# Moving the logits tile of the second layer from the attention's tile pool to the kept residual's pool

## The chip, the cores and the metric

The kernel is one launch on one core of a Trainium2 chip. The metric is device time in microseconds (us). TensorE is called PE (its weight loads PEld), VectorE DVE, ScalarE ACT, GpSimd POOL and SyncE SP. "L1098" is line 1098 of the kernel's source.

## The reference, cut to what matters

Two layers run over x, 2708 tokens of 256 floats, with a 2708 x 2708 adjacency matrix. Each layer is a graph attention followed by a top-2 mixture of 8 experts, both added to the residual. The change lies in the second layer:

```python
# layer 1, attention (x is the residual, Xn its layer norm)
H = Xn @ W_fc + b_fc
scores = where(adj > 0, s_src[:, None] + s_dst[None, :], -1e9)
x = x + softmax(scores) @ H
# layer 1, experts
xf = layernorm(x)
logits = xf @ gate_w + gate_b              # [2708, 8]
probs = softmax(logits); top2_vals, top2_idx = top_k(probs, 2)
for e in range(8):                          # hidden size 512
    y = gelu(xf @ W1[e] + b1[e]) @ W2[e] + b2[e]
    acc += weight_of(e) * y
x = x + acc
```

Since the row's own score s_src cancels in the softmax, the kernel weights row j of H with exp(s_dst[j]). And since the gate is linear, the gate's 8 columns are folded into the matrix of the attention: each value row carries its share of the logits, and the attention sums them with the rest.

## The kernel before, in words

Tokens are handled in 22 tiles t of 128 rows (the last has 20). Layer 0 ends with its experts, whose results are scattered into xd0 in memory. Then `layer1_attention` runs, and after it `experts1.run`.

**Attention of layer 1.** It opens a tile pool att1 (L585) on the left side of SBUF. In it lie parts (the value rows as three bf16 parts), logits (L589, 22 x 8 floats for each partition), spread_of, e_tail, sums_of and the working tiles xT, e, rest, m_tail. The residual rows lie in `kept`, in a pool of their own on the right side (L1226), which is open to the end of the kernel. While the first group of tiles is under way, every tile t gets its norm, its columns and its values; L624 writes the part of `logits[:, t]` that comes from the token itself. The 22 tiles are attended in groups of 6, 6, 4, 3 and 3 (GROUPS). When a group is done, L682 copies its sums out of PSUM to `raw`, and a generator `finish` (L665) for each tile is put into a list of open work, `line`. At L722 the loop ends; its pools are closed when `layer1_attention` returns, while the finishes of the last groups are still open in `line`.

**finish and route.** Each call of `line.step()` moves every open finish on by one step. Its steps for layer 1: divide by the sum (L234 to L239), add into kept (L670), add the attention's share to `logits[:, t]` (L673), norm statistics (L197 to L199, with a power on POOL in L203), the normalized row (L209), the scaled logits (L865, the last read of `logits[:, t]`), the two best experts (L870, L871), the softmax over them (L876, L877 on ACT), the one-hot sum `sel` (L887), two matmuls that count places (L891, L892), and two indirect DMAs from POOL which scatter the row to its experts (L909).

**Experts of layer 1.** Rows are worked off in slots of 128 rows of one expert, 47 here. After 16 routed tiles `begin` (L1020) places slots 0 to 23, and asks for rows and weights of the first three. The weights lie in a ring of four buffers, which were filled ahead with guessed experts; `fetch_weights` (L1047) is an indirect DMA from POOL whose indices are out of bounds, and move nothing, where the right expert is there already. A slot is `up` (L1085): two transposes of its rows to PSUM (L1088), a copy to `xe` (L1098), a copy of the bias (L1101), 16 matmuls (L1108), 4 Gelu (L1116); then `down` (L1121) of the slot before: 8 matmuls (L1124), y (L1130, L1131), and a scatter to xd1 (L1135). Between them stand two `line.step()`. When `line` is empty, `place(24, SLOTS)` lays out the remaining slots. The tiles xe, bias2, hT and y come from the pool ffn2, called two (L1074), which is opened on the right side after att1 is closed. Its PSUM pools (L1075 to L1077) take the banks of the attention's.

**What sets the order.** SP's instructions keep the order of the source. On the other engines, the tile framework lays out an order at build time: an instruction that is earlier in the source goes first if its inputs are there by the framework's own estimate of time. On the chip each engine then works through its list in that order, and waits on semaphores. A pool that takes the addresses of an earlier pool comes after it: in the built program, xe of slot 0 lies at bytes 147712 to 148736 of a partition, att1 at 112000 to 158144, and logits at 145408 to 146112. xe of slot 0 shares no byte with logits, yet its copy (L1098) carries a semaphore wait on the DVE's own count, and the value is that of L865 of tile 21.

Of the kernel before, what the change touches and what calls it, by code (L numbers as in the profile page):

```python
# [9 lines left out]
F32 = mybir.dt.float32  # L10
# [9 lines left out]
P = 128  # L20
# [3 lines left out]
E = 8  # L24
BN = 512
EPS = 1e-5
NT = (N + P - 1) // P
# [33 lines left out]
def adj_ffn_kernel(ctx: ExitStack, tc: tile.TileContext, a: dict, out: bass.AP):  # L61
# [521 lines left out]
    def layer1_attention(mTs, kept, line):  # L583
        with ExitStack() as scope:
            pool = scope.enter_context(tc.tile_pool(name="att1", bufs=2))  # L585
            ps_acc = scope.enter_context(tc.tile_pool(name="acc1", bufs=6, space=PSUM))
            parts = pool.tile([P, NT - 1, 3, VALUES + 1], BF16, name="parts", bufs=1)

            logits = pool.tile([P, NT, E], F32, name="logits", bufs=1)  # L589
            spread_of = pool.tile([P, NT], F32, name="spread_of", bufs=1)  # L590
            e_tail = pool.tile([P, VALUES + 1], F32, name="e_tail", bufs=1)
            sums_of = pool.tile([P, DC, NT], F32, name="sums_of", bufs=1)
# [623 lines left out]
    with tc.tile_pool(name="mask", bufs=1) as mp:  # L1216
        mTs = [
            mp.tile([P, NT, nb], FP8, name=f"mT{b}") for b, (_, nb, _) in enumerate(BLOCKS)
        ]
        background.extend(  # L1220
            partial(nc.sync.dma_start, mTs[b], neighbours[b][:]) for b in range(len(BLOCKS))
        )
        experts0.run(line)
        early_rows.close()

        kept_pool = ctx.enter_context(tc.tile_pool(name="kept", bufs=1, side="right"))  # L1226
        kept = kept_pool.tile([P, NT, D], F32, name="kept")
        layer1_attention(mTs, kept, line)
# [58 lines left out]
```

## Time and profile before

| what | value |
|---|---|
| device time, median of 3 runs | 1366.69 us (1365.86 to 1366.7) |
| device time of the profiled execution | 1365.33 us |
| its span from first to last instruction | 1363.6 us |
| PE busy in the span | 1251.6 us (92%) |
| DVE, POOL, ACT busy | 581.8, 413.1, 333.5 us |
| mean TensorE clock granted | 0.962 |
| last matmul of the attention (L661) ends | 1108.67 us |
| first expert matmul of layer 1 (L1108) starts | 1122.39 us |

Times of single instructions are counted from the span's start. In a timeline, a line gives start, duration, engine, source line, operation, output and inputs, count, and in brackets the idle time before it with what ended that. In a table of windows, each engine has its busy time in that stretch and the number of instructions; PEclk is the granted clock as a share of full speed. Since the profile is of one execution, sums of its durations are taken against its own 1365.33 us; the 1.7 us outside of the span stay as they are.

### The profile page before, as it was taken

To read this page: it belongs to the slowest core of one execution; us is meant where nothing else is said; L and a number is where in the kernel's file an instruction comes from. 1 tells how busy PE (TensorE), PEld (TensorE's weight loads), DVE (VectorE), ACT (ScalarE), POOL (GpSimd) and SP (SyncE) were. 2 spreads that over 40 slices of the span, in tenths; PEclk is the share of its full clock that TensorE was granted. 3 is DMA by queue.
4 is the path that set the end of the run, shared out by engine and by line. 5 is a ranking of instruction groups with operands and counts; after the bars stand their busy time and mean duration, and the time that the engine had idled before them with its cause. 6 is when DMAs were issued, how large, how long until landed. Compare 5 with 4: busy or idle time off the path is not lost. (4 is left out here: it accounts for less than half of the span.)

```text
span 1363.6 us, 21427 instructions
## 1 busy us (share of the span) xinstructions
PE 1251.6 (92%) x7536; PEld 975.8 (72%) x7536; DVE 581.8 (43%) x2261; ACT 333.5 (24%) x1008; POOL 413.1 (30%) x521
## 2 busy tenths in 40 slices
PE   7999999999999999999999999689999868999980
PEld 4666666666566666999999999567887637888860
DVE  5723743636427255512212222276636564333324
ACT  3222212212112223533333233134100003222220
POOL 5200110110111112533333333341144365544440
PEclk8899999999999999999999999889999879999995
DMA  7701355988928327375678454440010033536447
GB/s 215 248 5 40 117 168 132 257 226 222 251 74 186 98 95 283 73 241 157 183 250 292 118 165 130 108 176 1 1 48 29 30 104 122 176 101 226 156 156 252
DMA packets 106058, 201.39 MB, mean 148 GB/s; under 512 B 25633, under 2 KB 79990, under 8 KB 99418
## 3 DMA queue, kind: packets, MB, share of 16 engines
q1 hardware_dynamic: 75740, 109.41, 28.1%
q0 software_dynamic: 27392, 87.78, 20.3%
q10 hardware_dynamic: 2814, 2.77, 0.6%
q8 instruction: 62, 1.02, 0.3%
q14 instruction: 50, 0.41, 0.1%
HBM read 263.63 MB, written 66.12 MB: 242 GB/s over the span
## 5 line engine op out<-in xcount | busy, mean ns | idle before, releaser
L1124 PE MATMUL acc<-ring,hT 128*128 128x256 f32 x1096 | 272.4, 385 | 16.7 <-ACT hT L1116 9.4
L1108 PEld LDWEIGHTS mm<-xe,ring 128*128 128x128 f32 x2192 | 266.8, 195 | 17.3 <-issue 8.3
L1108 PE MATMUL mm<-xe,ring 128*128 128x128 f32 x2192 | 274.9, 280 | 4.4 <-DVE xe L1098 3.4
L1116 ACT ACTIVATE hT<-mm,ring 128x128 f32<-128x128 f32 x548 | 156.4, 369 | 358.6 <-issue 337.5
L1124 PEld LDWEIGHTS acc<-ring,hT 128*128 128x128 f32 x1096 | 194.3, 191 | 45.5 <-issue 13.2
L429 PE MATMUL s<-g,xnT 128*128 128x512 f32 x420 | 206.4, 607 | 6.0 <-DVE mT L441 6.0
L486 PE MATMUL acc<-v,p 128*128 128x257 f32 (+1 forms) x880 | 209.1, 389 | 0.0
L1130 DVE TENSOR_TENSOR y<-acc,bias 128x256 f32<-128x256 f32 x92 | 39.1, 425 | 323.3 <-PE acc L1124 317.6
L655 PE MATMUL acc<-parts,mT 128*128 128x265 bf16 (+1 forms) x1386 | 173.0, 281 | 0.4 <-DVE raw L682 0.3
L486 PEld LDWEIGHTS acc<-v,p 128*128 128x128 f32 (+1 forms) x880 | 153.0, 190 | 18.0 <-issue 0.8
L1049 POOL DMA_INDIRECT ring<-L_ffn_packed,weight_row x98 | 102.8, 1049 | 206.5 <-issue 92.0
L655 PEld LDWEIGHTS <-mT 128*128 128x128 fp8e4 (+1 forms) x1386 | 132.3, 98 | 45.9 <-issue 18.7
L203 POOL TENSOR_TENSOR ln_rs<-ln_rs,minus_half 128x2 f32<-128x2 f32 x88 | 68.1, 776 | 242.2 <-DVE ln_rs L199 210.9
L441 DVE TENSOR_SCALAR mT<-s 128x512 fp8e4<-128x512 f32 x105 | 72.0, 687 | 138.8 <-ACT p L440 138.7
L909 POOL DMA_INDIRECT disp<-row,to x88 | 87.5, 994 | 137.8 <-DVE to L906 52.8
L429 PEld LDWEIGHTS s<-g,xnT 128*128 128x128 f32 x420 | 76.1, 193 | 53.3 <-issue 42.7
L440 ACT ACTIVATE p<-s 128x512 f32<-128x512 f32 x105 | 62.2, 595 | 168.1 <-PE s L435 167.0
L1142 POOL DMA_INDIRECT xd<-y,xg x45 | 70.7, 1571 | 82.8 <-issue 34.8
L435 PEld LDWEIGHTS <-apart 128*128 128x128 fp8e4 x420 | 32.5, 98 | 60.4 <-issue 60.4
L324 DVE TENSOR_SCALAR apart<-adj 128x677 fp8e4<-128x677 int32 x80 | 40.8, 515 | 47.9 <-DMA adj<-in_adj_dram 47.6
L1135 POOL DMA_INDIRECT xd<-y,xg x47 | 47.2, 1004 | 24.0 <-issue 11.3
L877 ACT ACTIVATE p<-p 128x2 f32<-128x2 f32 (+3 forms) x44 | 9.1, 206 | 163.1 <-DVE p L876 85.2
(227 smaller groups left out, 1126.1 us busy)
## 6 DMA issues: line engine op xcount, KB each, us to landing
adj<-in_adj_dram SPq DMA_DIRECT2D x84, 338.5 KB
L_ffn_packed<-in_L_ffn_W_dram SPq DMA_DIRECT2D x16, 1024.0 KB
xg<-disp SPq DMA_DIRECT2D x98, 129.0 KB
L_ffn_packed<-in_L_ffn_W_dram SPq DMA_DIRECT2D x16, 512.0 KB
neighbours<-mT SPq DMA_DIRECT2D x5, 1408.0 KB
mT<-neighbours SPq DMA_DIRECT2D x5, 1408.0 KB
xin<-in_x_dram SPq DMA_DIRECT2D x42, 128.0 KB
ring<-L_ffn_packed SPq DMA_DIRECT2D x4, 1154.0 KB
```

Of the source, the lines that this page charges most:

```text
L203: nc.gpsimd.tensor_tensor(rs[:r, 1], rs[:r, 0], minus_half[:r], ALU.pow)
L429: nc.tensor.matmul(ps[:kr, :nb], xnT[:, c, k0 : k0 + kr], g[:, c, :nb], start=(c == 0), stop=False,)
L440: nc.scalar.activation(p[:kr, :nb], ps[:kr, :nb], AF.Exp, scale=1.0 / 16.0)
L441: nc.vector.tensor_scalar(mT[:kr, k, :], ps[:kr, :nb], -BIG / 2, None, ALU.is_gt, saturate=False,)
L486: nc.tensor.matmul(accs[j][:r], p[keys, q0 : q0 + r], v[keys, k, :], start=(k == 0), stop=(k == NT - 1),)
L655: nc.tensor.matmul(acc[:r], mT[:, k, j * P : j * P + r], parts[:, k, i], start=(k == 0 and i == 0), stop=False,)
L909: nc.gpsimd.indirect_dma_start(disp[:], bass.IndirectOffsetOnAxis(ap=to[:r, j : j + 1], axis=0), rows2[j][:r], None,)
L1049: nc.gpsimd.indirect_dma_start(w, None, packed[:], bass.IndirectOffsetOnAxis(ap=self.weight_row[:, s : s + 1], axis=0), bounds_check=E * P ...
L1108: nc.tensor.matmul(ps[:, i, :], w[:, c * hidden + f * P : c * hidden + (f + 1) * P], xe[:, c, :], start=(c == 0), stop=(c == DC - 1),)
L1116: nc.scalar.activation(hT[:, f, :], ps[:, i, :], AF.Gelu, bias=w[:, b1 + f : b1 + f + 1])
L1124: nc.tensor.matmul(ps, hT[:, f, :], w[:, w2 + f * D : w2 + (f + 1) * D], start=(f == 0), stop=(f == hc - 1),)
L1142: start = nc.gpsimd.indirect_dma_start(xd[:], at, y, None, bounds_check=N - 1, oob_is_err=False, compute_op=ALU.add)
```

## The change

One line: the tile of the logits is taken from the pool of kept, with the same shape and type. That pool has one buffer for each tile, and is on the right side of SBUF; 22 x 8 x 4 = 704 bytes of each partition move from the left side to the right. All reads and writes of logits stay what they are.

```diff
             ps_acc = scope.enter_context(tc.tile_pool(name="acc1", bufs=6, space=PSUM))
             parts = pool.tile([P, NT - 1, 3, VALUES + 1], BF16, name="parts", bufs=1)
 
-            logits = pool.tile([P, NT, E], F32, name="logits", bufs=1)
+            logits = kept_pool.tile([P, NT, E], F32, name="logits")
             spread_of = pool.tile([P, NT], F32, name="spread_of", bufs=1)
```

## The prediction

> **What bounds the kernel now.** I read the page first: PE is busy for 92% of the span, so only time in which PE stands, or runs at a low clock, can be won. Then I asked for busy time in stretches of 20 us around the end of the second attention, where the logits are last used.
>
> ```profile
> 1080.00:1100.00 20.00, 20.00 (x152) 11.28 (x150) 11.87 (x76) 1.48 (x8) 9.16 (x14) 1.00 0.10 34
> 1100.00:1120.00 20.00, 10.38 (x73) 5.80 (x72) 13.26 (x79) 0.68 (x3) 12.20 (x17) 0.76 0.41 135
> 1120.00:1140.00 20.00, 17.80 (x112) 16.50 (x112) 9.57 (x51) 6.35 (x21) 11.78 (x16) 0.82 0.22 67
> ```
>
> After the time come the busy times of PE, PEld, DVE, ACT and POOL, then the clock. PE works throughout until 1100, does half of the next 20 us, and comes back at a clock of 0.82. So there is a hole of some 10 us, with a slow start behind it. The timeline of PE shows its edges:
>
> ```profile
> 1110.29 0.66 PE L1088 MATMUL tp<-ident,xg 128*128 128x128 f32 x2 [1.45 <-DMA xg<-disp]
> ...
> 1113.63 0.17 PE L892 MATMUL misc<-seen,ones 128*128 128x8 bf16 x1 [1.89 <-DVE raw L239]
> 1121.74 0.17 PE L891 MATMUL misc<-sel,before 128*128 128x8 bf16 x1 [7.94 <-DVE sel L887]
> 1121.76 0.17 PE L892 MATMUL misc<-seen,ones 128*128 128x8 bf16 x1
> 1122.39 6.17 PE L1108 MATMUL mm<-xe,ring 128*128 128x128 f32 x32 [0.47 <-DVE xe L1098]
> ```
>
> Slot 0's rows are transposed by 1110.95, but its first matmul starts at 1122.39. The brackets blame sel of tile 19 for 7.94 us; the end of the hole is xe. The DVE's timeline says why xe is so late:
>
> ```profile
> 1117.44 0.41 DVE L209 TENSOR_SCALAR row<-kept,ln_mv,ln_rs 128x256 f32<-128x256 f32 x1 [2.29 <-POOL ln_rs L203]
> ...
> 1121.33 0.21 DVE L865 SCALAR_TENSOR_TENSOR lg<-logits,ln_rs,L_ffn_gate_b_b 20x8 f32<-20x8 f32 x1 [2.41 <-POOL ln_rs L203]
> 1121.47 0.21 DVE L887 TENSOR_TENSOR sel<-hot 128x8 bf16<-128x8 f32 x1
> 1121.61 0.39 DVE L209 TENSOR_SCALAR row<-kept,ln_mv,ln_rs 128x256 f32<-128x256 f32 x1
> 1121.93 0.41 DVE L1098 COPY xe<-tp 128x256 f32<-128x256 f32 x1
> ```
>
> The 20-row line is the last read of logits (tile 21). xe follows it as the built program demands: its wait is on just that L865. L865 waited for POOL's power, and POOL was full:
>
> ```profile
> 1108.73 1.07 POOL L1049 DMA_INDIRECT ring<-L_ffn_packed,weight_row  x1 [0.64 <-DVE raw L682]
> 1110.10 1.23 POOL L1049 DMA_INDIRECT ring<-L_ffn_packed,weight_row  x1 [0.30 <-issue]
> ...
> 1116.68 1.55 POOL L203 TENSOR_TENSOR ln_rs<-ln_rs,minus_half 128x2 f32<-128x2 f32 x2
> ...
> 1120.58 0.72 POOL L203 TENSOR_TENSOR ln_rs<-ln_rs,minus_half 20x2 f32<-20x2 f32 x1
> ```
>
> So today's order is POOL's power for tile 21, L865, release of att1, xe, expert matmuls. From there to 1329 the experts keep PE at about 18.4 of every 20 us; an earlier start moves the end of the kernel, as the tail (results scattered, read back, added, stored) hangs on the last slot.
>
> **What the Trainium skill says.** "TensorE: Matmul & The Clock Gate", section "What's actually happening": PE runs at half clock until it has been busy for some 3.4 us. The trace agrees in kind: the clock is 1.00 until 1110, 0.50 from 1112 to 1126, and 0.84 in the next 4 us. "ScalarE: Activation LUTs", section "What ACT_TABLE_LOAD costs": about 1283 ns for each switch, plus some 1380 ns of draining. The trace has the same 1283 ns; the drain isn't visible in it as a group. No page says when a tile pool's memory is free; that is a matter of the built program.
>
> **The change, part by part.**
>
> *Removed wait.* With logits elsewhere, att1's last users are the matmuls that read parts, m_tail and e_tail. The last (L661) ends at 1108.67, before slot 0's transposes. xe(0) is then bound by these, 1110.95. DVE has no gap from 1108.15 to 1115.15, so the copy comes between other instructions (each at most 0.48 us): done by about 1112. Its weights are there: the request of 1108.73 moved nothing (the DMA view has only small packets on POOL's queue until 1112). So the matmuls of slot 0 start at about 1112.0 instead of 1122.39; 10.4 us is the ceiling, 11 with the copy first in line.
>
> *What is late next: slot 1's weights.* The DMA view by microsecond has, on POOL's queue, 0.15 MB in 1112 to 1113, 0.43 MB in 1113 to 1114 and 0.60 MB in 1114 to 1116, in sum 1.18 MB, which is one ring buffer (128 x 2308 x 4 bytes). It starts a microsecond after the second request ends (1111.33): I take it that slot 1's guess was wrong. So slot 1 can't start before 1116.0. Slot 0's 16 matmuls at half clock take 3.6 us (15 of the 32 took 1122.39 to 1125.75), so to 1115.6; slot 1 from 1116.0 to 1119.5. From the end of slot 1's matmuls to the start of slot 2's there are 2.7 us before (1128.56 to 1131.25; transposes, half of down(0), Gelu). So slot 2 starts at 1122.2 instead of 1131.25: 9.0 us gained without new waits. The half clock is paid in both kernels; I give it no gain.
>
> *Routing of tiles 19 to 21 now lies beside slots.* (a) PE's L891 of tile 19 needs sel, which DVE gives at 1121.7, since POOL is no faster. If it stands right behind slot 1's matmuls, PE waits from 1119.5 to 1121.7: 2.2 us; if later, nothing. I take 1.3. DVE's y(0) and xe(2) queue behind L865 of tile 21 until 1121.5, and are needed at about 1121.5: nothing. (b) ACT did the three Exp (L877, at 1118.86, 1123.77, 1125.54) before its first Gelu, with one table load. Now they alternate: up to three switches there and back, 3 x 2 x 1.28 = 7.7 us (double with the drains of the page). ACT needs 1.15 of 3.85 us for each slot, so 2.7 us a slot are free and a Gelu is due only after the next slot's 2 us of matmuls. Bounds: 0 to 7.7; I take 0.7, since at most one Gelu at a time lies behind a switch. (c) POOL gets two more requests for each slot, 1.04 + 1.02 + gaps = 2.7 us, into a queue that is full until 1125. The routing scatters come later by up to three slots, 8 us; the next that needs them all is the placing of slots 24 on, in slot 5, and a weight request is made three slots (11.5 us) ahead. Nothing, if the order holds; bounds -3 to +4 us, as PE already loses about 5 us around that placing (slot 4 starts at 1138.98, slot 6 at 1153.53, for a pitch of 3.85).
>
> *Moved memory.* The first write of logits (L624) must now find kept's addresses free. kept's own first load comes earlier in the same pool, and DVE waited 8.7 us for it; L624's group shows 5.4 us of idle time, all but a trace of it for ACT's e. So nothing. Left and right sides shift by 704 bytes and stay clear of each other by the same gap. No instruction, DMA or queue entry is added; DVE, ACT and PE do the same work.
>
> Sum: 9.0 - 1.3 - 0.7 = 7.0 us. Against the profiled execution 1365.33 - 7.0 = 1358.3; its time is 1.4 below the median of the runs, so for the median 1366.69 - 7.0 = **1359.7**.
>
> **The rivals.**
> 1. *PE's order keeps the routing ahead of slot 1.* If the build places L891 of tile 19 before slot 1's matmuls, these start at 1121.8, end at 1125.2, slot 2 starts at 1127.9: 3.4 us gained, 1363.3. For it: the build does not know that slot 0's weights move nothing, so its estimate of weight arrival may be late. Against: slot 1 is earlier in the source, and PE is idle by then.
> 2. *The wait stays.* Some other late tile of att1, or the PSUM pools, holds two back; then 1366.7. Against: the wait of xe names L865 of tile 21, and only logits is read by finish and route from att1.
> 3. *Slower: ACT's queue.* An Exp stands before a Gelu and waits for its softmax input, which waits for POOL, now fuller by 2.7 us a slot. Each of three Exp then costs two switches with drains (5.3 us) and, with PE waiting for hT, up to 4 us of it are seen by PE: 12 against the 9 won, so 1369.7. It decides from 3 us seen per Exp. Against: 2.7 us of each slot are free on ACT.
> 4. *The hole around the placing closes too:* it costs 5 us now, and a different order may lose less; 1366.69 - 7 - 4 = 1355.7.
>
> **How the numbers follow.** Forecast 0.50, rival 1 0.25, rival 2 0.10, rival 3 0.10, rival 4 0.05. A measurement can tell about 0.2%, 2.7 us, from no change: faster are the forecast, rival 4 and most of rival 1 (3.4 lies close to the bound, so 0.03 of it goes to the middle), 0.77; same 0.13; slower 0.10. The range leaves out rivals 2 and 3: from 1355.5 (ceiling of 11 us, and rival 4) to 1365.5.
>
> **What would show it.** Right: xe(0) on DVE before the last L865, the first L1108 near 1112, slot 1 at 1116 to 1117, PE busy about 17 of 20 us in 1100 to 1120, more ACT table loads than the 10 of the groups before, the last matmul some 7 us earlier. Wrong: xe(0) still behind L865 (rival 2); L891 with a long idle bracket before slot 1 (rival 1); waits of L1124 for hT (rival 3); or a later stall around the placing that takes the gain back.

## The result and the profile after

| | kernel before | changed kernel |
|---|---|---|
| median of 6 runs each | 1366.7 us (1365.86 to 1369.49) | 1373.59 us (1369.48 to 1377.27) |
| ratio, with its 95% interval | | 1.0047 (1.0026 to 1.0067) |
| profiled execution, span | 1363.6 us | 1375.5 us |

The changed kernel is slower by about 6 us, where 7 us less were forecast. A second comparison on another chip (run e5 below) gave 1.0031 (1.0016 to 1.0045). The chips differ by some us, and single executions of one kernel on one chip by up to 16, so from here on times are compared as ratios to the kernel before on the same chip, and profiles from one fixed point: the end of the attention's last matmul (L661), which in the changed kernel's profile is at 1110.86 and in the one before at 1108.67.

What was forecast for the start of the experts came. DVE copies xe of slot 0 long before the last read of the logits:

```profile
1113.23 0.42 DVE L1098 COPY xe<-tp 128x256 f32<-128x256 f32 x1 [0.60 <-issue]
...
1138.95 0.20 DVE L865 SCALAR_TENSOR_TENSOR lg<-logits,ln_rs,L_ffn_gate_b_b 20x8 f32<-20x8 f32 x1
```

The windows show a full PE from 1100 to 1140 (16.82 against 10.38 in the first of these stretches), and then a hole in 1140 to 1160, where the kernel before had 16.30 us of PE:

```profile
1100.00:1120.00 20.00, 16.82 (x107) 10.71 (x105) 12.50 (x67) 1.82 (x3) 11.12 (x14) 0.83 0.43 138
1120.00:1140.00 20.00, 18.26 (x115) 16.88 (x116) 10.09 (x63) 9.20 (x27) 10.86 (x13) 0.91 0.17 48
1140.00:1160.00 20.00, 7.25 (x47) 5.87 (x45) 7.99 (x41) 3.55 (x8) 14.23 (x16) 0.82 0.52 168
```

PE's timeline has the start, the hole, and what follows it:

```profile
1114.78 3.62 PE L1108 MATMUL mm<-xe,ring 128*128 128x128 f32 x16
...
1121.09 0.41 PE L1088 MATMUL tp<-ident,xg 128*128 128x128 f32 x2 [2.34 <-DMA xg<-disp]
...
1121.37 3.24 PE L1108 MATMUL mm<-xe,ring 128*128 128x128 f32 x16
...
1160.75 3.78 PE L1124 MATMUL acc<-ring,hT 128*128 128x256 f32 x8 [12.11 <-ACT hT L1116]
...
1178.47 1.95 PE L1108 MATMUL mm<-xe,ring 128*128 128x128 f32 x16
1180.26 0.38 PE L1088 MATMUL tp<-ident,xg 128*128 128x128 f32 x2
1180.93 1.99 PE L1124 MATMUL acc<-ring,hT 128*128 128x256 f32 x8 [0.29 <-issue]
1182.76 0.27 PE L1088 MATMUL tp<-ident,xg 128*128 128x128 f32 x1
1182.87 1.95 PE L1108 MATMUL mm<-xe,ring 128*128 128x128 f32 x16
```

Two things are to be seen here. One is loud: 12.11 us before the down of slot 6. The other is quiet: after the hole each down (L1124) stands right behind its own up (L1108) and waits for the Gelu, 0.29 to 0.51 us in every slot, and the pitch of the slots (the time from one slot's start to the next) is 4.3 to 4.4 us. The page shows the loud part, not the quiet one. The first line is the group of the down in the kernel before, the second in the changed one:

```profile
L1124 PE MATMUL acc<-ring,hT 128*128 128x256 f32 x1096 | 272.4, 385 | 16.7 <-ACT hT L1116 9.4
```

```profile
L1124 PE MATMUL acc<-ring,hT 128*128 128x256 f32 x1096 | 273.0, 386 | 29.0 <-ACT hT L1116 22.9
```

The idle time for hT grows from 9.4 to 22.9 us, and 12.11 us of that is the one hole. The order of PE's list shows in the pitch.

POOL's timeline shows a changed order. Slot 4's weights go into the buffer of slot 0. Their request now stands ahead of the powers of tiles 19 and 20 (L203), and waits for slot 0's down, so the powers come at 1129.42 and not at 1116.68:

```profile
1117.85 0.98 POOL L909 DMA_INDIRECT disp<-row,to  x1 [0.31 <-issue]
1127.05 1.04 POOL L1049 DMA_INDIRECT ring<-L_ffn_packed,weight_row  x1 [8.22 <-PE acc L1124]
...
1129.42 1.42 POOL L203 TENSOR_TENSOR ln_rs<-ln_rs,minus_half 128x2 f32<-128x2 f32 x2
```

From there to 1158 POOL sends one indirect request after the other, and in the middle of that SP's eight stores of the placing take 16.21 us from 1143.89 on (6.33 before).

To see where the lead went, I took from each profile the starts of the slots (first of the 16 matmuls L1108), counted from the end of L661. Runs e1 to e18 are told below; e1 has the engine order of the kernel before in these slots, e5 is the changed kernel again.

The lead of a kernel at a slot is how much earlier that slot starts than in the kernel before.

| start of slot | before | e1 | changed | e5 | e11 serial | e9 | e10 |
|---|---|---|---|---|---|---|---|
| 2 | 22.6 | 22.6 | 16.2 | 13.6 | 22.3 | 13.5 | 22.5 |
| 4 | 30.3 | 30.3 | 24.1 | 21.4 | 30.0 | 20.7 | 30.6 |
| 6 | 44.9 | 39.3 | 35.7 | 36.4 | 45.1 | 33.5 | 40.9 |
| 8 | 52.6 | 46.7 | 58.9 | 52.7 | 54.6 | 51.1 | 50.8 |
| 12 | 68.3 | 62.2 | 76.3 | 70.1 | 71.8 | 68.9 | 67.0 |
| 24 | 120.1 | 114.1 | 128.5 | 122.3 | 123.2 | 116.5 | 115.9 |
| end of PE | 224.4 | 218.4 | 234.2 | 227.9 | 228.3 | 218.5 | 217.5 |

At slot 4 the changed kernel is 6 to 9 us ahead of the kernel before in its two profiles. At slot 8 it is 6 behind in the first and level in e5; at slot 12 it is 8 and 2 behind, and it loses 1 to 2 us more from there to the end. So nearly all is decided in slots 4 to 11.

### The profile page after: what moved, and what is told of

It reads as the page before. It is cut to its first block, busy times and chain, and to the rows that moved or that the text cites. A ratio compares the mean times of both kernels' runs of the same rounds, so it can differ in the third digit from the quotient of the medians.

```text
span 1375.5 us, 21421 instructions
## 1 busy us (share of the span) xinstructions
PE 1253.2 (91%) x7536; PEld 978.4 (71%) x7536; DVE 581.6 (42%) x2261; ACT 338.9 (25%) x1012; POOL 412.9 (30%) x521
## 5 line engine op out<-in xcount | busy, mean ns | idle before, releaser
L1124 PE MATMUL acc<-ring,hT 128*128 128x256 f32 x1096 | 273.0, 386 | 29.0 <-ACT hT L1116 22.9
L1108 PE MATMUL mm<-xe,ring 128*128 128x128 f32 x2192 | 276.7, 281 | 2.9 <-DVE xe L1098 2.9
L1108 PEld LDWEIGHTS mm<-xe,ring 128*128 128x128 f32 x2192 | 268.3, 196 | 15.4 <-issue 7.1
L1124 PEld LDWEIGHTS acc<-ring,hT 128*128 128x128 f32 x1096 | 195.8, 192 | 60.2 <-ACT hT L1116 28.6
L486 PEld LDWEIGHTS acc<-v,p 128*128 128x128 f32 (+1 forms) x880 | 154.3, 192 | 18.3 <-issue 0.8
L203 POOL TENSOR_TENSOR ln_rs<-ln_rs,minus_half 128x2 f32<-128x2 f32 x88 | 67.8, 773 | 244.4 <-DVE ln_rs L199 213.1
L846 POOL COPY row<-token 128x1 int32<-128x1 int32 (+1 forms) x88 | 17.1, 207 | 101.1 <-DMA disp<-row,to 99.8
```

Source lines behind the costliest of these rows:

```text
L203: nc.gpsimd.tensor_tensor(rs[:r, 1], rs[:r, 0], minus_half[:r], ALU.pow)
L486: nc.tensor.matmul(accs[j][:r], p[keys, q0 : q0 + r], v[keys, k, :], start=(k == 0), stop=(k == NT - 1),)
L1108: nc.tensor.matmul(ps[:, i, :], w[:, c * hidden + f * P : c * hidden + (f + 1) * P], xe[:, c, :], start=(c == 0), stop=(c == DC - 1),)
L1124: nc.tensor.matmul(ps, hT[:, f, :], w[:, w2 + f * D : w2 + (f + 1) * D], start=(f == 0), stop=(f == hc - 1),)
```

## The experiments

The first theories were: **A**, the early start brings the placing and POOL's late routing scatters together; **B**, the moved addresses cost by themselves; **C**, ACT's alternation of Exp and Gelu; **D**, POOL's burst alone.

**e1: the old wait put back.**

```diff
-            logits = kept_pool.tile([P, NT, E], F32, name="logits")
+            logits = kept_pool.tile([P, NT, E], F32, name="logits"); experts1.gate_bias = pool.tile([P, E], F32, name="bias_copy", bufs=1); nc.vector.tensor_copy(experts1.gate_bias, gb_b)
```

> The changed kernel, with the old wait put back by other means: L865 adds a copy of the gate's bias that lies in att1 (one DVE copy of 128x8 more), so the attention's pool is again free only after L865 of tile 21, while logits stays in kept's pool. Theory A (the loss comes from what the earlier start of the slots does to the order of the work around the placing of slots 24 on): the old order comes back and with it the old time, 1366.7 within 2. Theory B (the 704 bytes that moved, so other addresses of kept and of the pools on the right, cost time by themselves): it stays near 1373.6. Theory C (ACT's Exp and Gelu alternate and their table loads cost it): as A, 1366.7.

Measured: 0.9992 (0.9974 to 1.0009). Slot 0 starts 13.8 us after L661, as before (13.7). So the addresses cost nothing (B falls), and the whole difference hangs on the one wait.

**e2, e3: the placing in slot 10.** In the kernel before (e2) and in the changed one (e3):

```diff
-                if not placed and (not line.busy() or s + AHEAD == n):
+                if not placed and (not line.busy() and (own_norm or s >= 10) or s + AHEAD == n):
```

> The kernel before, with the second layer's slots 24 on placed in slot 10 and not in slot 5: SP's eight stores of L935 come some 20 us later, away from the last routing scatters of POOL; nothing else is moved on POOL or ACT. Theory A (these stores and the chain of the placing meet the routing scatters, and that is what stalls PE, ACT and DVE): the 5 us that PE loses at 1140 to 1154 mostly go, 1362 to 1364. Theory B and theory C (addresses, or table loads): nothing there to gain, 1366.7 within 1.5.

> The changed kernel, with the second layer's slots 24 on placed in slot 10 and not in slot 5; POOL's and ACT's order is that of the changed kernel to the last instruction. Theory A: the stall of 12 us before slot 6's down goes, SP's eight stores take about 6 us again, and the 7 to 9 us that the slots are ahead are kept: 1359 to 1362. Theory B (addresses): 1373 as before the edit. Theory C (table loads of ACT): they are as many as in the changed kernel, so 1372 to 1374. A fourth reading, theory D (POOL's 22 indirect DMAs back to back are enough to stall the others, the placing is not needed for it): a hole of 8 to 12 us stays at 1145 to 1160 with no store of SP near it, 1370 to 1373.

Measured: e2 1.0052 (1.0032 to 1.0073), e3 1.0054 (1.0036 to 1.0073). Theory A's numbers were missed in both: the late placing makes the kernel before slower, which no theory had. e3's time is what C had forecast (1372 to 1374 on the scale of 1366.7), so C was still open here. D's hole at 1145 to 1160 did not come. Slots 5 to 12 go smoothly there, but the cost comes back at slot 13. The timelines of e2 for SP and PE show why:

```profile
1162.93 7.78 SPq L935 DMA_DIRECT2D disp<-nobody  x8
1172.33 7.47 SPq L1064 DMA_DIRECT2D xg<-disp  x5
```

```profile
1179.05 0.66 PE L1088 MATMUL tp<-ident,xg 128*128 128x128 f32 x2 [3.24 <-DMA xg<-disp]
```

SP works off its list in order, and slot 13's row fetch stands behind eight stores. With the placing in slot 5, PE of the kernel before waits for no rows behind them. In e3 the 12 us hole is gone and slot 6 starts 6.3 us ahead of e1 (33.0 against 39.3), but slots 6 to 12 take 4.5 us each where e1 takes 3.8: the lead melts without any hole. That was the first sign of the quiet part.

**e4: all routing ahead of the first slot** (one line: `line.gap = 1; own_norm or line.finish()`, and the placing held in slot 5 by `s >= 5` in the condition above).

> The changed kernel, with all open routing written out in the source ahead of the first slot, and the placing kept in slot 5: on POOL the powers and scatters of tiles 19 to 21 then stand ahead of the weights of slots 4 to 6 and of the first scatters to xd1, so that no routing scatter is left when the placing comes. Theory A: no stall around the placing, but PE waits for sel of tile 21 near its first slots again or keeps them ahead, whichever the built order gives: 1359 to 1364. Theory B: 1373. Theory C (Exp all ahead of the Gelu, so few table loads): 1360 to 1364 too, so this run does not tell A from C; the one before it does. Theory D: POOL has the same number of indirect DMAs, a few less in one row: 1366 to 1373.

Measured: 1.0019 (1.0001 to 1.0037), slower than A and C had it and within D's range. Slot 2 starts only at 18.3 (12.8 in e3), since PE now waits for the routing, and slots 8 to 12 are again at 4.2 us each.

After this I held two theories: **P**, POOL's list is the bound once the slots start early; **S**, the hole alone, with the standstill in it (single steps of SP that take 0.7 us, told in the last section).

**e5, e6, e7, e8.** e5 is the changed kernel again. e6 and e7 leave the last six routing scatters out, in both kernels; their rows are missing from the experts, and neutral rows are laid there at the start of the kernel, which is the price of this test in both:

```diff
-            for j in range(2):
+            for j in range(0 if logits is not None and t >= 19 else 2):
                 self.other_rows(
...
+    for e in range(E): [nc.scalar.dma_start(disps[1][e * CAP + i * P : (e * CAP + (i + 1) * P), :], nobody) for i in range(3, 8)]
+    for a0 in (19 * P, 20 * P, N - P): [nc.scalar.dma_start(xd1[j * N + a0 : j * N + a0 + P, :], nobody[:, :D]) for j in range(2)]
```

e8 puts four steps of the routing ahead of the slots (`own_norm or [line.step() for _ in range(4)]`, placing held in slot 5).

> The changed kernel once more, with a new profile, beside the kernels below. In the first profile PE stood 12.1 us before slot 6's down while SP's register steps took 0.7 us each. Theory P (POOL's list is the bound as soon as the slots start early: the lead of 9 us over the kernel before melts from slot 4 to slot 12 on requests for weights that POOL makes late, and the placing then costs its 4 to 5 us in the open): the lead is 8 to 10 us at slot 4, under 4 us at slot 10, with or without the standstill; time 1.003 to 1.007 of the kernel before. Theory S (the standstill alone cost it): where it is missing, the lead of 7 us or more stays to the end, and the time is 0.994 to 0.997.

> The changed kernel without the six routing scatters (L909) of tiles 19 to 21, 8 us of POOL's list; their rows are left out of the experts, and 46 plain stores at the start of the kernel lay neutral rows in their place, so the total is read only against the twin below. Theory P: POOL no longer falls behind, so slot 8's weights are asked for 8 us earlier than in the changed kernel, and of the 9 us of lead over the twin at slot 4 at least 6 are left at slot 12 and at the end: 5 to 9 us faster than the twin. Theory S or a bound on the weights' transfer itself (4 us a slot): the lead melts all the same, under 3 us at the end.

> The kernel before with the same six scatters left out and the same 46 stores at the start: the twin of the last one. Theory P: little is gained by it here, since POOL had caught up in the 10 us in which PE stood: within 3 us of the kernel before, apart from what the stores at the start cost (0 to 10 us, the same in both twins). Theory S: the same.

> The changed kernel with four steps of the open routing written out ahead of the first slot (and the placing kept in slot 5): on POOL the powers of tiles 19 to 21 and four of the scatters then stand ahead of the request for slot 4's weights, where POOL stood idle for 4.7 us in the changed kernel because that request waits for slot 0's down. Theory P: those 4.7 us are filled, slot 8's weights are asked for 3 to 5 us earlier, and 3 to 5 us come off the changed kernel's time: 0.998 to 1.003 of the kernel before. Theory S: as the changed kernel, 1.003 to 1.007.

Measured: e5 1.0031 (1.0016 to 1.0045); e6 1.0259 (1.0227 to 1.0290); e7 1.0186 (1.0158 to 1.0215); e8 1.0031 (1.0016 to 1.0047). The lead in e5 went as P had it (8.9 us at slot 4, none at slot 10); S it does not test, since the standstill came again. The stores at the start cost e7 25 us, where at most 10 were expected. Less work on POOL did not help the changed kernel: e6 is 0.7% slower than its twin e7, about as much as with the scatters, or more, where P had it 5 to 9 us faster. So P falls as the main cause. e8 is at e5's time, as S had it and at the very edge of what P had; PE waits 4.72 us there for the place count (L922), and slot 4 starts only at 33.3. What e6 and e7 differ in is the pitch: from slot 8 to slot 17 e7 takes 3.7 us a slot, e6 4.3. Both have the same PE work and the same requests; so I compared the order of PE's list in the built programs (u5 is the up of slot 5, 16 matmuls L1108; d5 its down, 8 matmuls L1124; a d that stands twice is split by the u between):

```
before:   ... u4 d3 d4 u5 d4 d5 u6 u7 d6 d7 u8 d8 u9 d8 d9 u10 d9 d10 u11 d10 d11 u12 d12 u13 d13 ...
changed:  ... u4 d3 d4 u5 d4 d5 u6 d6 u7 d7 u8 d8 u9 d9 u10 d10 u11 d11 u12 d12 u13 d13 ...
e7:       ... u4 d3 d4 u5 d4 d5 u6 u7 d6 d7 u8 d8 u9 d8 u10 d9 d10 u11 d10 ... u19 d18 d19 u20 d20 ...
```

In the kernel before, most downs up to slot 10 stand at least in part behind the next slot's up, so PE has work while ACT does the Gelu. In the changed kernel the build wrote u, d, u, d from slot 6 on. That is theory **O**.

**e9, e10, e11, e12: the order forced.** e9 (changed kernel) and e10 (kernel before) get one ordering edge for each slot, which adds no instruction:

```diff
-                            nc.tensor.matmul(
+                            self.last_up = nc.tensor.matmul(
...
-                    nc.tensor.matmul(
+                    first = nc.tensor.matmul(
                         ps, hT[:, f, :], w[:, w2 + f * D : w2 + (f + 1) * D],
                         start=(f == 0), stop=(f == hc - 1),
-                    )
+                    ); f or own_norm or tc.add_manual_dep(first.ins, self.last_up.ins.name, mybir.DependencyInfo(mybir.DependencyClass.NoSync, mybir.DependencyReason.DATA), reason="order")
```

e11 is the kernel before with the reverse edge from slot 6 on (each up behind the down of the slot before, which is also written ahead of it in the source); its list reads `u5 d4 d5 u6 d6 u7 d7 ...`. e12 is e9 with the placing in slot 10.

> The changed kernel with one ordering edge for each slot of the second layer: the first matmul of a slot's down may stand in PE's list only behind the last matmul of the next slot's up. POOL's, ACT's and SP's lists stay as they are. Theory O (the order that the build writes down for PE is what took the gain back: in the changed kernel every down from slot 6 on stands right behind its own up and waits for the Gelu, 4.3 to 4.5 us a slot, where the kernel before overlaps them to slot 11 at 3.8): all slots run at 3.8 to 3.9 us, so 1350 to 1357 scaled to a kernel before of 1366.7, and 5 us or more faster than the same edge in the kernel before. Theory P (POOL's requests are the bound): 4.2 us a slot or more remains, within 3 us of the changed kernel without the edge, and not faster than the edge in the kernel before.

> The kernel before with the same ordering edge for each slot. Theory O: it gains the 0.4 to 0.5 us of each slot from 12 on, some 33 slots: 12 to 16 us faster than the kernel before, and 5 us or more slower than the changed kernel with the edge, since the lead of 9 us at slot 4 is then lost nowhere but at the placing. Theory P: the gain is under 5 us, since the weights can't come faster, and both kernels with the edge take the same time.

> The kernel before with the other order forced on PE: from slot 6 on, each down right behind its own up and ahead of the next up, as the build wrote it down in the changed kernel. Theory O: slots 6 to 11 take 4.3 to 4.5 us in place of 3.8, so 2.5 to 4.5 us slower than the kernel before, which is a good part of what the changed kernel lost. Theory P: POOL's list is nearly that of the kernel before and has slack, so no difference beyond 1 us.

> The changed kernel with the ordering edge and the placing in slot 10 and not in slot 5. If the placing in slot 5, where it meets POOL's late routing scatters, costs about 9 us by itself as the profiles of the changed kernel suggest, and 4 to 5 us in slot 10: 3 to 6 us faster than the edge alone. If the placing costs the same wherever it stands, within 1.5 us of the edge alone.

Measured: e9 0.9949 (0.9929 to 0.9968); e10 0.9952 (0.9934 to 0.9970); e11 1.0042 (1.0025 to 1.0060); e12 0.9979 (0.9964 to 0.9994).

e11 carries the weight here. POOL, ACT and SP go through the same list in its profile as in that of the kernel before, instruction by instruction. The old wait is in it, the experts start late (13.35 us after L661), and its hole at the placing (3.24 us for hT, ahead of slot 5's down) is much that of the kernel before (2.47); with the order of slots 6 to 11 alone it is as slow as the changed kernel. Its 5.7 us are somewhat more than the 2.5 to 4.5 that O had; P had at most 1. PE's timelines of e11 and e9 show what the order is worth in a quiet stretch:

```profile
1174.43 1.95 PE L1108 MATMUL mm<-xe,ring 128*128 128x128 f32 x16
1176.21 0.38 PE L1088 MATMUL tp<-ident,xg 128*128 128x128 f32 x2
1176.88 1.99 PE L1124 MATMUL acc<-ring,hT 128*128 128x256 f32 x8 [0.29 <-issue]
1178.71 1.95 PE L1108 MATMUL mm<-xe,ring 128*128 128x128 f32 x16
```

```profile
1165.05 1.95 PE L1108 MATMUL mm<-xe,ring 128*128 128x128 f32 x16
1166.83 1.89 PE L1124 MATMUL acc<-ring,hT 128*128 128x256 f32 x8
1168.56 0.38 PE L1088 MATMUL tp<-ident,xg 128*128 128x128 f32 x2
1168.78 1.39 PE L1108 MATMUL mm<-xe,ring 128*128 128x128 f32 x11
```

4.28 us from up to up in the first, 3.73 in the second: with the next up between, the Gelu is covered. On the page of e10 the group of the down has lost its idle time (16.7 us before), but the group of the up has 16.1 us, where the kernel before has 4.4; half of that is for the copy xe:

```profile
L1124 PE MATMUL acc<-ring,hT 128*128 128x256 f32 x1096 | 267.4, 382 | 2.9 <-ACT hT L1116 2.9
```

```profile
L1108 PE MATMUL mm<-xe,ring 128*128 128x128 f32 x2192 | 278.2, 281 | 16.1 <-DVE xe L1098 7.9
```

So e10 gains 6.6 us (4.1 to 9.0), where O had 12 to 16. Its slots 12 to 24 take 4.1 us each, against 4.3 before and 3.8 to 3.9 forecast.

The second half of O's forecast was missed too: with the same order on both sides the changed kernel is not faster (0.9949 against 0.9952), though its slot 4 starts 10 us earlier. That both take the same time was P's forecast. So the order accounts for the 6 us on the wrong side, and something else for the loss of the lead. In e9, slots 4 to 8 take 30.4 us, in e10 20.1. e9's PE waits there for the place count, for weights, for issue and for rows:

```profile
1138.75 0.17 PE L922 MATMUL misc<-seen,ones 128*128 128x8 bf16 x1 [2.07 <-DVE seen L900]
...
1141.26 3.79 PE L1108 MATMUL mm<-xe,ring 128*128 128x128 f32 x16 [1.06 <-DMA ring<-L_ffn_packed,weight_row]
...
1157.69 1.09 PE L1088 MATMUL tp<-ident,xg 128*128 128x128 f32 x4 [1.95 <-DMA xg<-disp]
```

The placing in slot 10 (e12) does not cure it: 28.2 us for the same slots, and slower than e9 in all, against both of its forecasts.

**e13 to e16: what takes the lead.** With the edge in both kernels, e13 and e14 leave out the six late scatters as in e6 and e7; e15 and e16 leave out the placing's eight register loads and stores on SP (`for e in range(E if self.own_norm else 0)`), with the same neutral rows laid at the start.

> The changed kernel with the ordering edge, and without the six routing scatters (L909) of tiles 19 to 21 (left out, with 46 plain stores of neutral rows at the start of the kernel, as in the twins before; to be read only against its own twin). If POOL's late scatters take the lead of 10 us away between slots 5 and 8: 5 to 9 us faster than its twin, slots 5 to 8 at 4 to 5 us each. If the placing's stores do: no more than 2 us faster than its twin.

> The twin: the kernel before with the ordering edge, the six scatters left out and the same stores at the start. POOL has caught up here before slot 4 in either theory, so it stands to the kernel before with the edge as the cost of the stores at the start alone (25 to 30 us, as measured in the earlier twins).

> The changed kernel with the ordering edge, and without the eight register loads and stores (L930, L935) of the second layer's placing on SP; neutral rows are laid there by the 46 stores at the start. If the placing's stores take the lead away between slots 5 and 8: 5 to 9 us faster than its twin, no row fetch late at slot 7 or 8. If POOL's scatters do: no more than 2 us faster than its twin, and the hole between slots 5 and 8 stays.

> The twin: the kernel before with the ordering edge, without the eight register loads and stores of the placing, and the same stores at the start. If the stores cost in this order too (slots 4 to 7 take 15.6 us there, 3 above their pitch), it is up to 3 us faster than the other twin of the kernel before.

Measured: e13 1.0221 (1.0196 to 1.0245) and e14 1.0269 (1.0239 to 1.0299), so the changed kernel is at 0.995 of its twin (the twin is the kernel before with the same edits); e15 1.0224 (1.0191 to 1.0257) and e16 1.0282 (1.0252 to 1.0312), at 0.994 of its twin. Taking the two intervals of a pair as independent, each of these has a half width of 0.004: both are just clear of 1. Slots 4 to 8 take 24.1 us in e13 and 21.9 in e15, against 30.4 in e9 and 18.5 in both twins. So the changed kernel keeps part of its lead with either cut, 5 to 9 us as forecast for the one that is the cause; the expectations had it as one or the other. Two forecasts were missed: e16 is not faster than e14, and e14 lies some 43 us above e10, not 25 to 30, so the cost of the stores at the start differs from kernel to kernel, and only pairs measured side by side say anything. What is left in e13 is a wait for weights, which POOL asked for late; first PE, then POOL, of e13:

```profile
1181.75 3.78 PE L1108 MATMUL mm<-xe,ring 128*128 128x128 f32 x16 [4.96 <-DMA ring<-L_ffn_packed,weight_row]
```

```profile
1173.10 1.09 POOL L909 DMA_INDIRECT disp<-row,to  x1 [0.31 <-issue]
...
1174.70 1.08 POOL L1049 DMA_INDIRECT ring<-L_ffn_packed,weight_row  x1 [0.16 <-PE misc L892]
```

The request for slot 6's weights goes out at 1174.70 behind scatters of earlier tiles, and from request to landing it takes 2.1 to 8.2 us here.

**e17, e18: all the work, but the stores spread out.** The edge, and the placing's stores given out one for each slot from 8 to 15 (its arithmetic stays in slot 5), in the changed kernel and in the one before:

```diff
-                for e in range(E):
+                def neutral(e, end=end):
                     at = nc.values_load(
...
-                line.step()
+                line.step(); [self.neutral.pop(0)() for _ in range(len(self.neutral) if s + AHEAD + 1 == n else min(s > 7, len(self.neutral)) if placed else 0)]
                 behind = (s, w, xg, hT, bias2)
```

> The changed kernel with the ordering edge, and with the eight stores of the second layer's placing given out one for each slot from slot 8 to slot 15 in place of all at once in slot 5; the placing's arithmetic stays in slot 5, nothing is left out. If the meeting of the stores with POOL's late scatters takes the lead: the standstill between slots 6 and 8 goes, 5 us or more faster than the edge alone (0.9949), so 0.990 or less of the kernel before, and the fastest of all versions. If the stores cost the same wherever they are, or POOL alone takes the lead: 0.993 to 0.997.

> The kernel before with the same two edits: here the scatters are through before the stores come, so little is to be won: within 2 us of the edge alone, 0.993 to 0.997 of the kernel before, and 4 us or more slower than the changed kernel with the same edits if the meeting is the cause, within 2 us of it if not.

Measured: e17 0.9958 (0.9940 to 0.9976), e18 0.9952 (0.9930 to 0.9975). No gain over the edge alone, and no difference between the two, as forecast for the case that the meeting of stores and scatters is not the cause. In e17 slots 4 to 8 take 26.4 us, 4 less than in e9, but 8 more than in e18 (18.4), and both lose time at slot 12 (the step from 11 to 12 takes 9.3 and 8.0 us) to row fetches behind the stores on SP. PE's timeline of e17:

```profile
1142.92 0.17 PE L922 MATMUL misc<-seen,ones 128*128 128x8 bf16 x1 [2.02 <-DVE seen L900]
...
1145.29 3.78 PE L1108 MATMUL mm<-xe,ring 128*128 128x128 f32 x16 [0.82 <-DMA ring<-L_ffn_packed,weight_row]
1148.87 2.83 PE L1124 MATMUL acc<-ring,hT 128*128 128x256 f32 x8
...
1154.85 0.27 PE L1108 MATMUL mm<-xe,ring 128*128 128x128 f32 x1 [1.76 <-issue]
1156.26 0.95 PE L1108 MATMUL mm<-xe,ring 128*128 128x128 f32 x7 [1.14 <-issue]
```

Here the lead goes in small parts: 1.14 us for sel of a late tile (L891, at 1135.81), 2.02 us for the place count of the last tile (its routing, late through POOL, now lies in the midst of the slots), 0.82 for weights, 2.8 for the up of slot 6 and the down of slot 5, slow after these waits (3.78 and 2.83 us against 1.95 and 1.89), 2.9 in a standstill of issue.

This limits what e15 says. In e12 and e17, too, no store of the placing falls in slots 4 to 8 (the first comes 52.5 and 50.7 us after L661), and these slots take 28.2 and 26.4 us, against 21.9 in e15. So stores in these slots are not the main thing that takes the lead, and why e15 keeps some of it stays open.

**The fastest versions** are e9 and e10, at 0.995 of the kernel before; they don't differ. The edge is what pays, and moving the logits adds nothing to it.

## Why the prediction was wrong, point by point

- **The wait that is removed: right.** It hung on L865 and nothing else, and went with the tile (e1 puts it back, and the time with it). Rival 2 is out. Slot 0's matmuls start 3.9 us after L661; 3.3 were forecast (1112.0 less 1108.67).
- **What is late next: right in size in e5, 2.6 us short in the first profile, and not in place.** Slot 1 was limited not by its weights but by the fifth pair of transposes (L1088). The pairs come in the order of the slots, so it is slot 4's; it stands ahead of slot 1's matmuls in PE's list and waited 2.34 us for its rows. Slot 2 started 6.4 us earlier in the first profile and 9.0 in e5, against 9.0 forecast.
- **(a) PE and sel, 1.3 us: wrong place.** L891 of tile 19 did not come ahead of slot 1 (rival 1 is out) but within slot 4, without a wait. The price was paid later, at the place count L922: 1.00 us in the first profile, 2.38 in e5 (where another L891 waits 0.78 as well).
- **(b) ACT's tables, 0.7 us: about right.** Four loads lie between 1133 and 1144.4, and PE's waits for hT beside them are 0.64 and 0.39 us. Rival 3 had the sign of the result, but not its mechanism: e9 has the list of ACT of the changed kernel to the last instruction, and is faster than the kernel before. What the loads cost of the lead was not measured by itself.
- **(c) POOL and the placing: the step that failed.** It said "Nothing, if the order holds; bounds -3 to +4 us". The order did not hold, on two engines. On POOL, the request for slot 4's weights moved ahead of the powers of tiles 19 and 20, so the last routing fell among slots 4 to 8. There, late weights and rows, the place count, the low clock after each hole and the standstill took 10 us (e9 against e10, from slot 4 to slot 8): all of the lead. The direction is the same in all seven pairs of profiles with equal edits (e2 with e3, e6 with e7, and so on): the changed kernel takes 3 to 13 us more for these slots. The bound of 4 us was too small by more than half. The 5 us named there as today's loss around the placing were mis-added as well: from 1138.98 to 1153.53 are 14.55 us, 6.9 more than two slots of 3.85.
- **The step that was missing.** The sum let each slot after slot 2 keep its pitch. PE's list was rewritten by the build as well: u, d, u, d from slot 6 instead of slot 12. e11 prices that alone at 1.0042, 5.7 us (3.4 to 8.2). The profiles show 3.3 us of it: slots 6 to 12 take 26.7 us in e11 and 23.4 in the kernel before. The rest of the 5.7 they don't place.
- **Moved memory: right**, nothing (e1).
- **Rival 4** (a different order may lose less around the placing) is out: it lost more.

Put together: -9 from the start, +10 between slots 4 and 8 with equal order, and +6 for PE's order, give a loss of about 7 us; 6.4 were measured, and 4.2 in e5. Shown by runs are the wait (e1), the order (e11, e9, e10), and that the whole lead is lost with equal order (e9 and e10 take the same time). That it is lost in slots 4 to 8 is read from profiles. Not settled is why: without the late scatters (e13) part of it lasts, but so does part without the stores (e15), while moving the stores (e12, e17) keeps none of it in the time. How the 10 us divide among the waits named, and what makes the standstill, stays open.

That the early profiles, before and changed, differ by 2.2 us ahead of the change is chance: the end of L661 lies between 1107.7 and 1115.2 in the executions of kernels that do the same work up to there.

## What to carry to other kernels

When a wait goes, the build can write a new order for other engines, also far from the edit, as it did here for PE, DVE, ACT and POOL: before adding up what becomes free, ask what each in-order queue will hold in place of the old list, and price the pitch of the loop behind it, not only its start. A gap on the engine that sets the end can be another engine's time to catch up, as here POOL finished the routing while PE stood. And where a matmul waits for an activation of its own step, one ordering edge that puts the next step's matmuls between can be worth more (0.5% here) than the wait that caught the eye.

## What the runs showed of the hardware that was not expected

- **A standstill of issue on several engines at once.** In the changed kernel, between 1147 and 1160, single register steps of SP (0.03 us each elsewhere) took 0.7 us, and its eight stores 16.21 us; in e9 at the same place PE issued single matmuls of 0.27 us at distances of 1.4 us, with nothing named as the cause. The DMA engines were not full (0.28 and 0.32 busy in 1145 to 1155 of e9). It came again in e5 (the eight stores took 11.90 us) and, shorter, in e10, the kernel before with the edge (a step of 1.40 us, the stores 8.98). In e12 it came at 1154 to 1157, where SP's stores came from 1166 on; e3, e13 and e15 show none of it.
- **After a hole PE pays twice.** The 16 matmuls of an up took 3.78 or 3.79 us behind the waits around slot 6 (e9, e13, e17) against 1.95, with the clock granted at 0.50 in that stretch of e9. In e13 the 4.96 us of waiting cost another 1.83 in the up and 0.80 in the down (2.69 against 1.89).
- **The same lists don't give the same profile.** The kernel before and e1 have the same order of ups and downs in these slots, and the step from slot 5 to slot 6 took 8.4 us in one execution and 4.7 in the other. One profile is not enough for a cause of this size; the ratios above rest on 5 to 22 runs each.
